# A gated graph layer on one Trainium2 core: the last pair's products reordered, and four loads moved to other places in their queues

## The chip, the cores and the metric

The kernel runs on one core of a Trainium2 chip, in float32. The metric is the device time of one execution in microseconds; the time of a version is the median of its runs. The core has a matrix engine (PE, with PEld for its weight loads), VectorE (DVE), ScalarE (ACT), GpSimd (POOL) and a sync engine (SP) that only issues transfers. SP, ACT and POOL each issue DMAs from their own instruction streams. In this program the transfers of SP and ACT share eight semaphores in rotation: each of them waits, before it is issued, for the landing of the eighth transfer before it. The transfers of POOL have eight of their own.

## The reference, cut to what matters

There are 32 samples of 512 nodes with 256 channels, and a symmetric 0/1 adjacency of 512 x 512 for each.

```python
h = maximum(layernorm(x), 0)                       # per node
xc = transpose(h)                                  # channels x nodes
c = relu(bn1(conv1d(xc, conv1_w)))                 # 1 tap, 256 -> 256
x_conv = relu(bn2(conv1d(c, conv2_w, pad 8)) + xc) # 17 taps, 256 -> 256
s = h @ w_se.T + b_se                              # 3 features a node
A = exp(-|s_n - s_m|^2) * adj
x_nmp = A @ relu(h @ w_msg.T + b_msg)
gi = concat(x_conv, x_nmp) @ w_ih.T + b_ih ; gh = h @ w_hh.T + b_hh
r, z = sigmoid(gi_r + gh_r), sigmoid(gi_z + gh_z)
n = tanh(gi_n + r * gh_n)
out = x + (1 - z) * n + z * h
```

## The kernel before, in words

The samples are worked in two groups of 16, and the gates in 16 pairs after both.

*First part of a group* (`first_part`, L815). For each sample: the load of x (`load_x`, L116, 512 KB; the first sample's x_0 comes in four chunks of 128 KB, L945, by turns on the sync and ScalarE queues), layernorm statistics and normalisation on DVE (L280 to L304, with one power on POOL, L290), transposition on PE (`phT`, L311), the copy of it to DRAM (`hd`, L316), the one-tap convolution (`pc`, L327; DVE L330 makes its output `h`), and the transform of windows of 64 tokens to frequencies (`px`, L342). Between the samples of group 0 the 17-tap weights are transformed to frequencies: `taps`, a 40 KB matrix (its DMA is L133), stays in front of weights `w2p` (DMAs of L242, the first ones on the sync queue, the later ones on POOL's), the products `pw` (L255) are copied to `wst` (L265) and written to DRAM (`wd`). The order of all this is written out by hand (`manual_schedule`). The x of the sample three ahead is loaded at the top of each turn of the loop (L857) into one of three buffers. In group 0 it is on POOL's queue, together with `w2p`; on the sync queue stand the stores `hd` and `wd` and other loads.

*Nodes of a group* (`nodes`, L972). For each sample: message products (`pm`, L439, with DVE L441 and L442 behind them), features and their factors (`psl`, `psr`, `sl`, `sr`, L450 to L467), distances (`pd`, L476), exp on ScalarE (`e`, L479), the adjacency (`load_adj`, L408: four transfers of 256 KB on the sync queue) transposed on DVE in 32 x 32 blocks (`at`, L481), their product `A` (L482), and the aggregate `pn` (L491), which is saved to DRAM. Between them PE works the frequency units of the 17-tap convolution: unit u needs its weights `wt_u` (`load_unit`, L351, two transfers of 256 KB, L354, on the sync queue), their sum on POOL (`wsum`, L358), sums of the transformed input (`both`, L371 and L372, POOL) and makes `py` (L392), `y` (L395 to L400). In this stage the program's scheduler decides the order on each engine and which PSUM bank a tile gets, except for the stretches that are written out. The weights of units 0 to 2 of group 0 are loaded at the end of the first part (L966), ahead of the first adjacency (L984).

*Gates* (L1051 on). A pair's products are made with a scheme of seven products instead of eight, Q1 to Q7 in place of the 2 x 2 blocks of the gates' weights and the two samples: Q1, Q6, Q2, Q7, Q5, Q4, Q3 in this order, each in a PSUM bank of 512 columns, with sums on DVE and sigmoid on ScalarE as banks become ready. The order is written out by hand. For the last pair everything but the z gate's second half is done before; then `last_z` (L653) runs, and nothing comes after it. In it `into` (L601) makes a product, `gated` (L660, L662) adds a sum and takes the sigmoid, `turned` (L669, L672) multiplies with h - n and transposes to token order on DVE, `added` (L677) adds to the output tile, and `store` (L808) issues four transfers of 128 KB for a whole sample, or of 64 KB for half of its columns, by turns on the sync and ScalarE queues. Indices are (channel half, sample of the pair). Q5 and Q3 are computed in two halves of 256 columns, in banks of their own (`b3`); Q4 is computed in one piece in `b4`. Q5 gives the piece (1, 1), Q4 the piece (1, 0), Q3 the piece (0, 1).

Of the kernel before, what the change touches and what calls it, by code (L numbers as in the profile page):

```python
# [65 lines left out]
def gnn_layer(  # L66
# [15 lines left out]
    nc = tc.nc  # L82
# [43 lines left out]
    fwd_np, taps_np, back_np, spans = dft_constants(KT, N)  # L126
# [3 lines left out]
    w1 = early.tile([P, DC, D], FP, name="w1")  # L130
    fwd = early.tile([P, 2 * L], FP, name="fwd")
    taps = early.tile([P, ROWS], FP, name="taps")
    nc.scalar.dma_start(taps, nc.inline_tensor(taps_np, name="dft_taps").ap())  # L133
    back = consts.tile([P, back_np.shape[1]], FP, name="back")

    GC = G // P
# [212 lines left out]
    WT, WSUM, BOTH = {}, {}, {}  # L349
# [158 lines left out]
    Q1, Q6, Q2, Q7, Q5, Q4, Q3 = range(7)  # L508
# [89 lines left out]
    def into(bk, q, o, ks, terms, first, t=slice(0, N)):  # L598

        for i, k in enumerate(ks):  # L600
            nc.tensor.matmul(bk[:, t], sw[:, k, q, o, :], terms[k][q][:, t], start=(first and i == 0), stop=(i == len(ks) - 1),  # L601
                             skip_group_check=True)
# [50 lines left out]
    def last_z(p, terms):  # L653

        d, o, ks = RZ[p], 1, range(K3)

        def gated(src, other, i, j, t=slice(0, N)):
            z, g = d[:, DC + i, j, t], DC + i
            if other is not None:
                nc.vector.tensor_add(z, other[:, t], src[:, t])  # L660
                src = z
            nc.scalar.activation(z, src, AF.Sigmoid, bias=brz[:, g : g + 1], scale=1.0)  # L662

        def places(i, t):
            return slice(t.start // 32, t.stop // 32), slice(32 * i, 32 * (i + 1))

        def turned(i, j, t=slice(0, N)):
            dst, (js, half) = d[:, i, j, t], places(i, t)
            nc.vector.tensor_mul(dst, dst, d[:, DC + i, j, t])  # L669
            if (p, j) not in OUT:  # L670
                OUT[p, j] = pools["late"].tile([P, N // 32, D // 4], FP, tag="o", name=f"o_{p}_{j}", bufs=2)
            nc.vector.transpose(OUT[p, j][:, js, half], dst.rearrange("p (j k) -> p j k", k=32))  # L672

        def added(i, j, t=slice(0, N)):
            js, half = places(i, t)
            x = XP[p][j][:, js, half]
            nc.vector.tensor_add(x, x, OUT[p, j][:, js, half])  # L677


        ts = [slice(h * N // 2, (h + 1) * N // 2) for h in range(2)]  # L680
        b1, b2, b4, *b3 = (bank(f"pz{k}_{p}") for k in range(1, 6))
        into(b1, Q1, o, ks, terms, True)
        p1 = temp("p1", f"z{p}")
        nc.scalar.copy(p1, b1)
        into(b2, Q6, o, ks, terms, True)
        u2 = temp("u2", f"z{p}")
        nc.vector.tensor_add(u2, p1, b2)
        into(b1, Q2, o, ks, terms, False)
        gated(b1, None, 0, 0)
        early_out(p, 1, 1)  # L690
        turned(0, 0)
        into(b2, Q7, o, ks, terms, False)
        u3 = temp("u3", f"z{p}")
        nc.vector.tensor_add(u3, p1, b2)
        early_out(p, 0, 1)
        added(0, 0)
        for bk, t in zip(b3, ts):
            into(bk, Q5, o, ks, terms, True, t)
            gated(bk, u3, 1, 1, t)
        into(b4, Q4, o, ks, terms, True)  # L700
        turned(1, 1)
        added(1, 1)
        gated(b4, u3, 1, 0)
        for bk, t in zip(b3, ts):
            into(bk, Q3, o, ks, terms, False, t)
            gated(bk, u2, 0, 1, t)
            if t is ts[0]:
                turned(1, 0)
        added(1, 0)
        store(p, 0, [nc.sync, nc.scalar])  # L710
        for t in ts:
            turned(0, 1, t)
            added(0, 1, t)
            store(p, 1, [nc.sync, nc.scalar], t)
# [100 lines left out]
    def first_part(g, freq, between, left=()):  # L815


        b0, b1 = g * GB, (g + 1) * GB
        for b in range(b0, b0 + 3):
            if b not in X and (g == 0 or b == b0):  # L820
                load_x(b)
        if g == 0:
            t = XN[b0] = pools["first"].tile([P, NC, D], FP, tag="xn", name="rows", bufs=2)
            ones, diags = t[:, 0, :P], t[:, 1:3, :].rearrange("p i (c m) -> p i c m", m=P)
            nc.vector.memset(ones, 1.0)

            for _ in range(5):
                nc.tensor.matmul(row1[1][:, : 2 * P], ident, fr.rearrange("p c g k -> p (c g k)")[:, : 2 * P], start=True, stop=True)
            batch_norm("bn1", scale1, shift1, nc.gpsimd)
            bn1_row(0, scale1, ones, diags)  # L830
            bn1_row(1, shift1, ones, diags)
        if b0 not in STATS:
            statistics(b0)
        normalise(b0)
        if g == 0:
            scale_w1()
            shift_w1()
        left = list(left)

        def fill():  # L840
            for step in left.pop(0) if left else ():
                step()

        if g > 0:
            load_x(b0 + 1)
            fill()
            load_x(b0 + 2)
        transpose_h(b0)
        fill()
        statistics(b0 + 1)  # L850
        if g > 0:
            statistics(b0 + 2)
        normalise(b0 + 1, g > 0)
        fill()
        for b in range(b0, b1):
            if b + 3 < b1:
                load_x(b + 3, nc.gpsimd)  # L857
            if b == b0:
                conv1(b)
                one, two = between(0) if g == 0 else ([], [])  # L860
                for step in one:
                    step()
                fill()
                if g == 0:
                    transpose_h(b + 1)
                    statistics(b + 2)
                    normalise(b + 2)
                else:
                    normalise(b + 2)
                    transpose_h(b + 1)  # L870
                fill()
                xf, last_two = freq(g), two
                continue
            if g == 0:

                slots = last_two if b == b0 + 1 else between(b - b0)

                def slot():
                    for step in slots.pop(0) if slots else ():
                        step()  # L880

                if b == b0 + 1:
                    between(b - b0)
                    conv1(b)
                    slot()
                if b == b0 + 2:
                    slot()
                if b == b1 - 1:
                    load_h(b0)
                if b + 2 < b1:  # L890
                    statistics(b + 2)
                if b + 1 < b1:
                    transpose_h(b + 1)
                if b > b0 + 2:
                    slot()
                if b + 2 < b1:
                    normalise(b + 2)
                if b > b0 + 1:
                    conv1(b)
                    slot()  # L900
                if b == b1 - 1:
                    by_chunks(b)
                    load_h(b0 + 1)
                windows_to_freq(b - 1, xf)
                slot()
                continue
            if b + 2 < b1:
                statistics(b + 2)
            if b + 1 < b1:
                transpose_h(b + 1)  # L910
            if b + 2 < b1:
                normalise(b + 2)
            one, two = between(b - b0)
            conv1(b)
            if b == b1 - 1:
                load_h(b0)
            for step in one:
                step()
            windows_to_freq(b - 1, xf)
            for step in two:  # L920
                step()
        if g > 0:
            by_chunks(b1 - 1)
            load_h(b0 + 1)
        windows_to_freq(b1 - 1, xf)
        by_chunks(b0)
        return xf
# [8 lines left out]
    with tc.tile_pool(name="freq", bufs=1) as fpool:  # L936
# [3 lines left out]
        with phase("first", "gen"):  # L940
# [7 lines left out]
            load_w1()  # L948
            load_x(1)
            load_taps(gen, 0, nc.sync)  # L950
            nc.scalar.dma_start(fwd, nc.inline_tensor(fwd_np, name="dft_fwd").ap())

            def between(b):
# [9 lines left out]
            with tc.manual_schedule():  # L963
                xf = first_part(0, freq_tile, between)

                for u in range(3):  # L966
                    load_unit(0, u)


# [2 lines left out]
        def nodes(g, xf, units, last):  # L972
# [9 lines left out]
                    features(todo[i])  # L982

            load_adj(todo[0])  # L984
            with tc.manual_schedule():
                begin(0)
                message(todo[1], [0])
                factors(todo[0])
                message(todo[1], [1])
                features(todo[1])  # L990
# [133 lines left out]
```

## Time and profile before

Three runs took 1836.25, 1836.52 and 1836.99 us; the median is 1836.52. The profiled execution has a span of 1835.1 us.

| engine | busy, us | share | instructions |
|---|---|---|---|
| PE | 1814.2 | 99% | 6614 |
| DVE | 1108.7 | 60% | 2220 |
| POOL | 590.5 | 32% | 572 |
| ACT | 583.3 | 32% | 1084 |

The DMA engines moved 289.26 MB. In the first fortieth of the span PE has 8 tenths, in the last 7, in every one between them 9 or more; the DMA share is 8 or 9 tenths in the first seven fortieths (some 320 us), between 5 and 9 in the next twelve, and between 1 and 4 in the last twenty-one.

To read it: busy times are sums over the whole span. A stage's limit is seen in what each engine waited for and in the timeline, whose lines give the start, the length, the engine (with a q at the end for an engine's DMA issues), the line of the code, the operation, the tiles as output<-input and, in brackets, the idle time before and what ended it. A long DMA issue includes the time in which the queue waited for semaphores between several issues that are shown in one line. The columns of a window are the busy time of each engine with its number of instructions, then the clock that was granted to PE (1.00 is full), the mean busy share of the 16 DMA engines and the rate in GB/s.

### The profile page before, as it was taken

What the parts mean: (1) busy time and instruction counts of PE and PEld (TensorE: products, weight loads), DVE (VectorE), ACT (ScalarE), POOL (GpSimd) and SP (SyncE); (2) the same over time, 40 slices, a digit from 0 to 9 for tenths busy, and PEclk for the clock granted to TensorE, in tenths of its full rate; (3) what the DMA queues carried; (4) which work ended last, traced back from release to release, by engine and by line L of the source; (5) the groups of instructions that cost most, each with busy time, mean ns of one, the idle gap of its engine ahead of it and who ended that gap; (6) DMA issues with size and microseconds to landing.
All of it is one profiled execution on the core that took longest, in us unless ns stands there. A gap on an engine that the chain in (4) does not pass through costs nothing.

```text
span 1835.1 us, 20110 instructions
## 1 busy us (share of the span) xinstructions
PE 1814.2 (99%) x6614; PEld 1083.6 (59%) x6614; DVE 1108.7 (60%) x2220; ACT 583.3 (32%) x1084; POOL 590.5 (32%) x572
## 2 busy tenths in 40 slices
PE   8999999999999999999999999999999999999997
PEld 6777666666997766765545554555445554555443
DVE  7884565654995555454266556654666456655666
ACT  4556443432345343333212221222212221222121
POOL 3431333334432534444321332223221323133221
PEclk9999999999999999999999999999999999999999
DMA  9998889775669988767332344224422443234412
GB/s 249 306 299 225 238 225 254 199 208 182 209 225 220 261 249 222 232 194 245 103 111 60 71 121 121 82 38 121 120 87 44 110 121 105 57 79 121 121 27 43
DMA packets 307500, 289.26 MB, mean 158 GB/s; under 512 B 148076, under 2 KB 237196, under 8 KB 307012
## 3 DMA queue, kind: packets, MB, share of 16 engines
q1 hardware_dynamic: 281380, 224.22, 46.2%
q10 hardware_dynamic: 18992, 38.68, 5.9%
q0 software_dynamic: 7024, 25.07, 4.4%
q8 instruction: 53, 0.87, 0.2%
q14 instruction: 51, 0.42, 0.1%
HBM read 191.50 MB, written 96.40 MB: 157 GB/s over the span
## 4 chain that ended last, share of the span: by engine, by line
PE 65%; issue 1%; DVE 1%; POOL 1%; ACT 0%; DVEq 0%; POOLq 0%; ACTq 0%
PE pg L601 30%; PE pn L601 15%; PE pn L491 6%; PE py L392 6%; PE pc L589 5%; PE pm L439 2%; PE pd L476 1%; PE pz L601 1%; PE psr L465 0%; POOL cp L579 0%; POOL nt L791 0%; POOL rz L790 0%; DVE rz L669 0%; DVE o L672 0%; DVE xb L677 0%
## 5 line engine op out<-in xcount | busy, mean ns | idle before, releaser
L491 PE MATMUL pn<-A,msg 128*128 128x512 f32 x512 | 225.7, 593 | 1.2 <-ACT e L479 1.2
L601 PE MATMUL pg<-hp,sw 128*128 128x512 f32 x434 | 221.9, 593 | 0.7 <-DVE rz L620 0.5
L601 PE MATMUL pg<-cp,sw 128*128 128x512 f32 x434 | 221.7, 592 | 0.0
L601 PE MATMUL pg<-np,sw 128*128 128x512 f32 x434 | 221.7, 592 | 0.0
L579 POOL TENSOR_TENSOR hp<-hp 128x512 f32<-128x512 f32 x64 | 82.3, 1296 | 415.9 <-DMA hp<-hd 296.1
L371 POOL TENSOR_TENSOR both<-xf 128x256 f32<-128x256 f32 x78 | 60.6, 777 | 327.2 <-PE py L392 292.5
L491 PEld LDWEIGHTS pn<-A,msg 128*128 128x128 f32 x512 | 96.9, 190 | 111.5 <-issue 105.9
L579 POOL TENSOR_TENSOR cp<-cp 128x512 f32<-128x512 f32 x64 | 80.5, 1268 | 225.6 <-ACT cp L595 224.4
L392 PE MATMUL py<-wt,both 128*128 128x256 f32 x624 | 152.1, 387 | 0.3 <-ACT e L479 0.3
L616 ACT ACTIVATE rz<-rz,brz 128x512 f32<-128x512 f32 x93 | 67.0, 721 | 260.2 <-DVE rz L620 260.2
L399 DVE TENSOR_TENSOR y<-y,py 128x256 f32<-128x256 f32 x78 | 31.8, 408 | 186.6 <-ACT y L398 182.6
L601 PEld LDWEIGHTS pg<-hp,sw 128*128 128x128 f32 x434 | 82.4, 190 | 104.6 <-issue 97.7
L601 PEld LDWEIGHTS pg<-cp,sw 128*128 128x128 f32 x434 | 82.6, 190 | 103.7 <-issue 103.7
L601 PEld LDWEIGHTS pg<-np,sw 128*128 128x128 f32 x434 | 82.6, 190 | 103.7 <-issue 103.7
L392 PEld LDWEIGHTS py<-wt,both 128*128 128x128 f32 x624 | 114.9, 191 | 43.1 <-issue 28.3
L482 DVE TENSOR_TENSOR A<-e,at 128x512 f32<-128x512 f32 x128 | 114.5, 933 | 32.8 <-ACT e L479 32.6
L358 POOL TENSOR_TENSOR wsum<-wt 128x512 f32<-128x512 f32 x78 | 108.5, 1392 | 49.9 <-DMA wt<-wd 37.3
L739 ACT ACTIVATE nt<-nt,vech 128x512 f32<-128x512 f32 x64 | 46.2, 722 | 235.8 <-DVE nt L738 235.8
L327 PE MATMUL pc<-w,hT 128*128 128x256 f32 x512 | 117.9, 384 | 1.1 <-DVE hT L315 1.1
L439 PE MATMUL pm<-wmsg,hq 128*128 128x259 f32 x512 | 117.5, 382 | 0.0
L601 PE MATMUL pn<-hp,sw 128*128 128x512 f32 x224 | 114.4, 592 | 0.0
L601 PE MATMUL pn<-np,sw 128*128 128x512 f32 x224 | 114.4, 592 | 0.0
(145 smaller groups left out, 2946.4 us busy)
## 6 DMA issues: line engine op xcount, KB each, us to landing
wt<-wd SPq DMA_DIRECT2D x160, 256.0 KB, 4.4
adj<-in_adj_dram SPq DMA_DIRECT2D x128, 256.0 KB, 5.6
wd<-wst SPq DMA_DIRECT2D x64, 320.0 KB, 6.4
yd<-y ACTq DMA_DIRECT2D x80, 256.0 KB, 4.1
yt<-yd SPq DMA_DIRECT2D x30, 640.0 KB, 7.5
hd<-hT SPq DMA_DIRECT2D x32, 512.0 KB, 4.9
nd<-nmp ACTq DMA_DIRECT2D x32, 512.0 KB, 4.3
xb<-in_x_dram SPq DMA_DIRECT2D x128, 128.0 KB, 3.8
```

The costliest lines, as they stand in the source:

```text
L327: nc.tensor.matmul(p[:, j, :], HT[b][:, ic, c * P : (c + 1) * P], w1[:, ic, :], start=(ic == 0), stop=(ic == DC - 1))
L358: nc.gpsimd.tensor_tensor(t, WT[g, u][:, 0], WT[g, u][:, 1], op=ALU.add)
L371: nc.gpsimd.tensor_tensor(both[:, 0], re, im, op=ALU.add)
L392: nc.tensor.matmul(dst, v[:, ic, :], w[:, ic, :], start=(ic == 0), stop=(ic == DC - 1))
L439: nc.tensor.matmul(p[:, : D + NS], hq[:, ic, c * P : (c + 1) * P], wmsg[:, ic, :], start=(ic == 0), stop=(ic == DC - 1))
L482: nc.vector.tensor_mul(A[b][:, mc, :], e, at)
L491: nc.tensor.matmul(p, MSG[b][:, mc, dc * P : (dc + 1) * P], A[b][:, mc, :], start=(mc == 0), stop=(mc == NC - 1))
L579: nc.gpsimd.tensor_tensor(t[:, dst, :], t[:, a, :], t[:, b, :], op=sub)
L589: nc.tensor.matmul(bk[:, t0:t1], YT[p][j][:, c, oc * P : (oc + 1) * P], back[:, n : n + t1 - t0], start=(c == 0), stop=(c == len(spans) - ...
L601: nc.tensor.matmul(bk[:, t], sw[:, k, q, o, :], terms[k][q][:, t], start=(first and i == 0), stop=(i == len(ks) - 1), skip_group_check=True)
L616: nc.scalar.activation(rz[:, g, j, :], src, AF.Sigmoid, bias=brz[:, g : g + 1], scale=1.0)
L739: nc.scalar.activation(n, n, AF.Tanh, bias=b_in[:, i : i + 1], scale=1.0)
```

## The change

It has four parts.

1. In `last_z` Q4 is computed in front of Q5's two halves instead of behind them. The piece (1, 0) is turned after Q5's first half and added after Q5, and the first sample of the pair is stored there; the piece (1, 1) is turned after Q3's first half and added after Q3. The same instructions are issued in another order. Its purpose is to have the first sample of the pair complete earlier, so that its stores are not in front of the last ones.
2. The DMA of `taps` goes behind the two chunks of x_0 on ScalarE's queue, so that x_0 comes first.
3. The loads of x_3, x_4 and x_5 go from POOL's queue to the sync queue, where each stands between the stores of `hd`.
4. The weights of the third unit (`wt_2`) are loaded behind the first adjacency instead of in front of it. In group 1 they are there already and the condition is false.

In the nodes' stage of group 0 the scheduler's order changes with the fourth part: at its start DVE's work for `y_1`, `y_2` and the next sample's `st` and `msg` stands in front of the second adjacency's `at` and `A`, POOL's `wsum_2` behind `both_3`, and PSUM banks are given out otherwise, so that some `pd`, `py` and `pn` wait for other readers of their bank. The order of PE's instructions is the same in both but for `last_z`, and each engine has as many instructions as before, apart from the three loads.

```diff
@@ -130,7 +130,6 @@
     taps = early.tile([P, ROWS], FP, name="taps")
-    nc.scalar.dma_start(taps, nc.inline_tensor(taps_np, name="dft_taps").ap())
     back = consts.tile([P, back_np.shape[1]], FP, name="back")
@@ -694,20 +693,21 @@
         early_out(p, 0, 1)
         added(0, 0)
+        into(b4, Q4, o, ks, terms, True)
+        gated(b4, u3, 1, 0)
         for bk, t in zip(b3, ts):
             into(bk, Q5, o, ks, terms, True, t)
             gated(bk, u3, 1, 1, t)
-        into(b4, Q4, o, ks, terms, True)
-        turned(1, 1)
-        added(1, 1)
-        gated(b4, u3, 1, 0)
+            if t is ts[0]:
+                turned(1, 0)
+        added(1, 0)
+        store(p, 0, [nc.sync, nc.scalar])
         for bk, t in zip(b3, ts):
             into(bk, Q3, o, ks, terms, False, t)
             gated(bk, u2, 0, 1, t)
             if t is ts[0]:
-                turned(1, 0)
-        added(1, 0)
-        store(p, 0, [nc.sync, nc.scalar])
+                turned(1, 1)
+        added(1, 1)
         for t in ts:
             turned(0, 1, t)
             added(0, 1, t)
             store(p, 1, [nc.sync, nc.scalar], t)
@@ -854,7 +854,7 @@
             if b + 3 < b1:
-                load_x(b + 3, nc.gpsimd)
+                load_x(b + 3, nc.sync if b < 3 else nc.gpsimd)
@@ -948,6 +948,7 @@
             load_taps(gen, 0, nc.sync)
+            nc.scalar.dma_start(taps, nc.inline_tensor(taps_np, name="dft_taps").ap())
             nc.scalar.dma_start(fwd, nc.inline_tensor(fwd_np, name="dft_fwd").ap())
@@ -963,7 +964,7 @@
-                for u in range(3):
+                for u in range(2):
                     load_unit(0, u)
@@ -982,6 +983,8 @@
             load_adj(todo[0])
+            if (g, 2) not in WT:
+                load_unit(g, 2)
             with tc.manual_schedule():
```

## The prediction, made before the changed kernel was run

> **What bounds the kernel now.** I read the page's busy times first, then what TensorE (PE) waited for, then the timeline around each of those waits, then windows of 3.4 us for the clock, and last the timeline of the end.
>
> ```profile
> PE 1814.2 (99%) x6614; PEld 1083.6 (59%) x6614; DVE 1108.7 (60%) x2220; ACT 583.3 (32%) x1084; POOL 590.5 (32%) x572
> ```
>
> PE is busy 1814.2 of 1835.1 us. The other 20.9 us are all that reordering can give back, apart from matmuls that ran at a lower clock: 1.9 before the first matmul, about 8.1 in gaps, 10.9 after the last matmul has ended (1824.2). What PE waited for (total, times, longest):
>
> ```profile
> PE pn L491 <- ACT e L479: 1.2, 1, 1.2
> PE px L342 <- DVE h L330: 1.2, 1, 1.2
> PE phT L311 <- DVE xn L303: 1.2, 1, 1.2
> ```
>
> These are single events, all in the first 180 us. The second, from the timeline (start, length, engine, line, idle before):
>
> ```profile
> 20.25 0.81 POOL L118 DMA_DIRECT2D x<-in_x_dram  x1
> ...
> 30.70 1.40 DVE L284 BATCH_NORM_STATS2 stats<-x 128x6 f32<-128x256 f32 x4 [2.04 <-DMA x<-in_x_dram]
> ...
> 33.24 1.41 PE L342 MATMUL px<-fwd,h 128*128 128x160 f32 x8 [0.48 <-DVE hT L315]
> ...
> 35.85 1.41 PE L342 MATMUL px<-fwd,h 128*128 128x160 f32 x8 [1.20 <-DVE h L330]
> ```
>
> The fifth sample's load (x_4) is issued by GpSimd (POOL) at 20.25, lands at 30.67, and VectorE (DVE) stands 2.04 us in front of its statistics. DVE's later work is late by that, and PE waits 0.48 + 1.20 for it. The first wait of the list:
>
> ```profile
> 176.84 1.30 DVE L481 STREAM_TRANSPOSE at<-adj 128x512 f32<-128x512 f32 x2 [1.32 <-DMA adj<-in_adj_dram]
> ...
> 179.65 7.13 PE L491 MATMUL pn<-A,msg 128*128 128x512 f32 x16 [1.24 <-ACT e L479]
> ```
>
> The first adjacency's last quarter lands at 176.71, DVE waits 1.32 for it, and the chain transpose, exp, A, first aggregate brings 1.24 of it to PE. The windows behind (PE, PEld, DVE, ACT, POOL busy; then PEclk, DMA share, GB/s):
>
> ```profile
> 193.10:196.50 3.40, 2.72 (x11) 0.88 (x10) 3.40 (x15) 1.98 (x4) 0.73 (x1) 1.00 1.17 201
> 196.50:199.90 3.40, 3.40 (x10) 2.68 (x10) 3.40 (x5) 2.35 (x5) 0.72 (x2) 0.53 1.21 185
> ```
>
> In the second PE has a clock of 0.53: 3.4 x 0.47 = 1.6 us lost without being idle. The end:
>
> ```profile
> 1823.60 0.59 PE L601 MATMUL pz<-cp,sw 128*128 128x256 f32 x2
> 1824.05 0.69 DVE L669 TENSOR_TENSOR rz<-rz 128x512 f32<-128x512 f32 x1 [0.46 <-ACT rz L662]
> ...
> 1826.42 4.90 SPq L808 DMA_DIRECT2D out_dram<-xb  x6
> 1826.42 5.09 ACTq L808 DMA_DIRECT2D out_dram<-xb  x6
> ...
> 1828.52 0.42 DVE L677 TENSOR_TENSOR xb<-xb,o 128x256 f32<-128x256 f32 x1
> ```
>
> After PE's end DVE works without a break to 1828.94 and six stores on each queue follow.
>
> [...] all 16 DMA engines have a share of 0.9 to 1.0 from 10 to 40 us. [...] The 64 KB stores at the end take 2.7 to 4.3 us to landing. [...] The trace shows one window at half rate, [...] after a thin stretch (nine-row matmuls, a gap of 0.68).
>
> **The change part by part.**
>
> *Tail.* Same instructions, another order. PE goes on without a gap: Q4 (six matmuls of 512, 2.58 us) from 1816.28 to 1818.86, Q5's halves to 1820.15 and 1821.44, Q3's as before to 1822.73 and 1824.02. DVE: fourth add 1819.06 to 1819.75; first Q5 half added at 1820.8, its mul and transpose (1.00 + 0.71 for 512 columns at these lines[...]) to 1822.2; second half added at 1822.6; the output add (0.65) to 1823.2. In before that output add ended at 1826.39: the first sample's four stores leave 3.2 us earlier. Then come Q3's two adds (0.4 each) and, for three half-sized pieces, mul, transpose and add (0.42 + 0.45 + 0.43, with issue 1.4 each): DVE has no rest from 1822.6, and its last add ends near 1828.5 instead of 1828.94, that is 0.4 earlier. The last stores gain more. Before, they were issued at 1830.1 to 1831.2, up to 2.3 us after their data, since each transfer of the two hardware queues waits for the landing of the eighth before it, and the first sample's stores had left only at 1826.4 to 1827.7. Now those land by about 1827.5, before 1828.5. The last issue, second of two in a row on its queue (0.45 each), then starts near 1829.0 and lands 2.7 to 3.5 later, at 1831.7 to 1832.5 instead of 1833.9; the end came 1.2 after that landing. Gain 1.4 to 2.2; I take 1.8. The added costs: two store issues on ScalarE (0.39 + 0.46) now stand in front of Q3's two sigmoids, which then end near 1824.6 and 1826.0, while DVE comes to them at 1826.1 and 1827.4: nothing. PE's second Q3 half needs DVE's read of the second Q5 half, 1822.6 against PE's 1822.73: nothing, by 0.1.
>
> *Taps behind x.* One issue of 0.46 leaves ScalarE's front; chunks 1 and 3 of x_0 land 0.45 earlier (4.50 and 5.64 before). The first layernorm chain follows, but at 14.05 PE waits for the taps' weights w2p from the sync queue, which don't move. Gain 0.1 to 0.4; 0.2. Taps itself, 40 KB wanted at 14, is hidden.
>
> *x_3 to x_5 on the sync queue.* POOL loses three issues (1.00, 0.81, 0.80), off the path. x_4 stands behind the second hd store (issue about 18), 2 us earlier than now and in front of the 128 KB w2p that preceded it on POOL. Landing between 25 and 30, as 512 KB shares full engines; DVE wants it at 28.65. So of the 1.68 us on PE, 0.3 to 1.68 goes; I take 1.4. New wait: x_5 now stands behind the hd store of 27.22, so leaves at about 28.5 instead of 25.93, and lands near 36 instead of 33.38, while its statistics are wanted at about 34.5 once x_4 is on time. DVE then stands 1.5 to 2.3 us; behind it are transposes and PSUM copies for a PE that has 2 to 3.7 us of such work ready. Cost 0 to 1; 0.3. Head together: -0.2 - 1.4 + 0.3 = -1.3 (-2.0 to -0.1). From 40 to 165 us PE has no gap, though DVE stands up to 1.72 there, so shifts in that stretch cost nothing.
>
> *Adjacency in front of the third weights.* Two transfers of 256 KB, some 1.3 us each by the distance between the adjacency's landings (172.86, 174.18, 175.54, 176.71), move behind. The last quarter lands at about 174.1, and DVE is then bound by its own work, which ends at 175.51: 1.32 earlier, so PE's 1.24 go. The third weights land at about 176.7 instead of 171.5; POOL wants them at about 178, PE at 187: free. -1.2.
>
> *The scheduler's side effect.* In that stage DVE now does the y sums and the next sample's msg before the second adjacency's transposes, and PSUM banks are dealt otherwise: distance (pd), y and aggregate matmuls wait for other readers. From the end of the second message batch (193.43) to the next aggregate (200.61) before took 7.18. With the new order I count two small gaps (0.25 and 0.95, on exps) instead of 0.68, and no half-rate window: 4.9. [...] half of -2.3: -1.1.
>
> Sum: -1.8 - 1.3 - 1.2 - 1.1 = -5.4; with the median before of 1836.5 this gives 1831.1, rounded to 1831.0.
>
> **Rivals.** *Only the certain half*: tail -1.8, adjacency -1.2, head -0.1 (x_5 takes back what x_4 gives, PE waits for w2p), no gain at 193: -3.1, 1833.4, inside 0.2%. For it: DMA engines are full in the head[...]. Against: x_4 was late by its place in the queue, and that is mended. *All of it*: head -2.0, adjacency -1.2, tail -1.9, 193 us -2.3: -7.4, 1829.1. For it: [...] gaps get smaller. Against: new gaps at the same place. *Slower*: the tail's early end is worth its 0.4 only[...]; x_5's stall reaches PE in full (+2); the new bank order stalls PE on exps in several samples and each thin stretch is followed by a half-rate window (+1.6 each, three of them): +6.4 in all with adjacency and tail off, about 1841.5. For it: one such window is in the trace. Against: DVE is busy 60%, and from 204 us on PE waits next to nothing.
>
> **How the numbers follow.** Forecast 0.52, certain half 0.26, all of it 0.16, slower 0.06. 0.2% is 3.7 us: under 1832.85 is faster. The forecast's spread crosses that bound now and then (0.05), the certain half is mostly same: faster 0.74, same 0.20, slower 0.06. The range reaches from all of it (1829.0) to just over the certain half (1834.0).
>
> **What would show it.** Right: DVE's output add for the first sample ends near 1823.2 before the end's shift, last stores without waiting, 9 us from PE's last matmul to the end; px without waits at 33 and 36; pn's first wait gone; PEclk 1.0 at 196. Wrong: a DVE stall on x_5 that is followed by a PE gap, PE waits at py or pd near 195, a new window at half rate, or the last stores landing as long after the last add as before.

## The result and the profile after

The changed kernel takes 1832.05 us (median of 6 runs, 1828.42 to 1835.48); the kernel before 1836.81 (6 runs). The ratio is 0.9971 with an interval of 0.9958 to 0.9984: 5.3 us faster, between 2.9 and 7.7. Taken a second time it was 1830.34 against 1836.32, ratio 0.9964 (0.9950 to 0.9977). The prediction of 1831.0 lies between both times.

Single runs of one version differ by several us, so a part worth one or two us does not show by time alone. I therefore took the span apart at four events of PE that are in the same place of its order in every version: the first distance product `pd`, the first aggregate `pn`, the second sample's `pn`, and the end of PE's last matmul ("PE's end" below). Worked out from the times in the traces (us, the kernel before and the changed kernel in two profiles each, the second ones from the runs further down):

| stretch | before | before, again | after | after, again |
|---|---|---|---|---|
| start to first pd | 167.29 | 165.87 | 166.42 | 165.32 |
| first pd to first pn | 12.36 | 13.05 | 12.65 | 12.64 |
| first pn to second pn | 20.96 | 20.91 | 18.63 | 19.62 |
| second pn to PE's end | 1623.59 | 1623.23 | 1624.25 | 1622.85 |
| PE's end to the end | 10.88 | 10.83 | 8.05 | 8.16 |
| span | 1835.08 | 1833.89 | 1830.01 | 1828.59 |

The page's busy times after:

```profile
PE 1815.0 (99%) x6614; PEld 1083.9 (59%) x6614; DVE 1107.4 (61%) x2220; ACT 583.8 (32%) x1084; POOL 588.6 (32%) x569
```

PE's work is what it was (1814.2 before); what shrank is the rest, from 20.9 to 15.0 us. What PE waited for after the change (total, times, longest):

```profile
PE pd L475 <- ACT sr L466: 1.0, 1, 1.0
PE pn L490 <- DVE A L481: 0.9, 1, 0.9
PE pc L326 <- DVE hT L314: 0.8, 2, 0.5
PE pw L254 <- DMA w2p<-in_w2T_dram: 0.7, 1, 0.7
```

All three waits that the prediction shows of before are gone. In their place stand one for `sr` that was 0.62 before, one for `A` at 860 us that the first profile of before does not have, and one for `w2p` at 13.3 us, which the prediction named as what eats the earlier x_0. The head's timeline, in which the load at 28.29 is that of x_5 (x_4's left at 17.54 and landed at 26.37):

```profile
28.29 1.29 SPq L118 DMA_DIRECT2D x<-in_x_dram  x1
29.01 1.39 DVE L283 BATCH_NORM_STATS2 stats<-x 128x6 f32<-128x256 f32 x4
...
34.80 2.44 PE L341 MATMUL px<-fwd,h 128*128 128x160 f32 x16
```

No stall in front of x_4's statistics and none in front of `px`. Yet the stretch to the first pd is only 0.9 shorter. The windows show one reason, a stretch at half clock at 28.0 (PE, PEld, DVE, ACT, POOL busy, then PEclk, DMA share, GB/s):

```profile
24.59:28.00 3.41, 3.41 (x16) 1.59 (x16) 3.38 (x13) 3.07 (x8) 1.01 (x1) 1.00 1.02 335
28.00:31.41 3.41, 3.41 (x13) 2.96 (x12) 3.38 (x13) 0.00 (x0) 0.38 (x1) 0.50 0.97 284
164.53:167.94 3.41, 2.40 (x15) 1.18 (x14) 1.46 (x9) 3.41 (x9) 0.00 (x0) 1.00 1.07 332
167.94:171.35 3.41, 3.41 (x12) 2.87 (x11) 0.00 (x0) 1.60 (x4) 1.27 (x1) 0.50 1.25 190
```

The stretch at half clock that stood at 196.7 us before is not there; two others are, at 28.0 and 167.9, the second of them behind the first pd. In the first aggregate's timeline the wait for the adjacency is gone from the first line, and the gap from the second:

```profile
176.29 1.31 DVE L480 STREAM_TRANSPOSE at<-adj 128x512 f32<-128x512 f32 x2
...
179.07 7.03 PE L490 MATMUL pn<-A,msg 128*128 128x512 f32 x16
```

The end:

```profile
1820.11 0.68 DVE L676 TENSOR_TENSOR xb<-xb,o 128x512 f32<-128x512 f32 x1
...
1820.81 5.96 SPq L808 DMA_DIRECT2D out_dram<-xb  x6
1820.81 0.94 ACTq L808 DMA_DIRECT2D out_dram<-xb  x2
...
1821.36 0.59 PE L600 MATMUL pz<-cp,sw 128*128 128x256 f32 x2
...
1824.72 2.13 ACTq L808 DMA_DIRECT2D out_dram<-xb  x4
...
1825.49 0.43 DVE L676 TENSOR_TENSOR xb<-xb,o 128x256 f32<-128x256 f32 x1
```

The first sample's stores now leave at 1820.81, 1.1 us ahead of PE's last matmul's end (1821.95), not 2.2 behind it. By the issue and landing times of the transfers, the last of them starts at 1826.37, 0.45 behind the end of the last add, and not at 1831.19, 2.25 behind it; from there to landing it takes as long as before (2.6 and 2.7).

### The profile page after: what moved, and what is told of

The parts are those of the page before. It is cut to its first block, busy times and chain, and to the rows that moved or that the text cites. A ratio compares the mean times of both kernels' runs of the same rounds, so it can differ in the third digit from the quotient of the medians.

```text
span 1830.0 us, 20109 instructions
## 1 busy us (share of the span) xinstructions
PE 1815.0 (99%) x6614; PEld 1083.9 (59%) x6614; DVE 1107.4 (61%) x2220; ACT 583.8 (32%) x1084; POOL 588.6 (32%) x569
## 4 chain that ended last, share of the span: by engine, by line
PE 65%; issue 1%; DVE 1%; POOL 1%; ACT 0%; DVEq 0%; POOLq 0%; ACTq 0%
PE pg L600 30%; PE pn L600 15%; PE pn L490 6%; PE py L391 6%; PE pc L588 5%; PE pm L438 2%; PE pd L475 1%; PE pz L600 1%; PE psr L464 0%; DVE A L481 0%; POOL cp L578 0%; POOL nt L791 0%; POOL rz L790 0%; DVE at L480 0%; DVE o L671 0%
## 5 line engine op out<-in xcount | busy, mean ns | idle before, releaser
L600 PE MATMUL pn<-cp,sw 128*128 128x512 f32 x224 | 114.4, 592 | 0.0
```

## The experiments

### Each part alone

The kernel before with the changed `last_z` (the first part of the change as shown above), with the adjacency in front, with x on the sync queue, and with taps behind x_0:

```diff
@@ tail
+        into(b4, Q4, o, ks, terms, True)
+        gated(b4, u3, 1, 0)
...
+        added(1, 0)
+        store(p, 0, [nc.sync, nc.scalar])
@@ adjacency
-                for u in range(3):
+                for u in range(2):
...
             load_adj(todo[0])
+            if (g, 2) not in WT:
+                load_unit(g, 2)
@@ x
-                load_x(b + 3, nc.gpsimd)
+                load_x(b + 3, nc.sync if b < 3 else nc.gpsimd)
@@ taps
-    nc.scalar.dma_start(taps, nc.inline_tensor(taps_np, name="dft_taps").ap())
...
             load_taps(gen, 0, nc.sync)
+            nc.scalar.dma_start(taps, nc.inline_tensor(taps_np, name="dft_taps").ap())
```

> The kernel before with the new order of the last pair's z gate alone. Theory: from the end of PE's last matmul to the end of the program 8.1 us, as in the changed kernel, instead of 10.9; everything ahead of it as before, so 1836.5 - 2.8 = about 1833.7, ratio 0.9985. Rival: the stores' landing in the changed kernel was helped by the other parts (fewer transfers, other phases), and the order alone brings only the earlier last add, 0.4 to 0.8 us: about 1835.9.

> The kernel before with the first adjacency in front of the third weights alone. Theory: PE's gap of 1.24 in front of the first aggregate goes, and from the second message batch to the second aggregate 0.4 to 0.7 us of gaps go too: 1.7 us less by gaps, about 1834.8. A further 1.6 comes or goes with each stretch of 3.4 us at half clock, which need not sit at 196.7 us any more. Rival: the reordered VectorE work and the other PSUM banks cost as much as the gap, and the saving at 193 to 200 us in the changed kernel was only the absence of the half-rate stretch: 1.2 less at most by gaps, about 1835.3.

> The kernel before with x_3, x_4 and x_5 on the sync queue alone. Theory: VectorE's 2.04 us wait for x_4 at 28.7 shrinks under 1 and PE's gaps of 0.48 and 1.20 at 33 and 36 us go; 1.0 to 1.7 less if no stretch at half clock falls into the first 40 us: about 1835.1. Rival: x_5, now behind the store of hd, makes VectorE wait over 1.5 us at about 35 us, and the gap only moves: 1836.5.

> The kernel before with the taps' matrix behind x_0 alone. Theory: layernorm of the first sample 0.4 to 0.8 us earlier, but PE waits for w2p at 14.0 us as before, so PE's gain by 14.1 us is below 0.1: 1836.5, no change. Rival: the earlier first sample reaches the second sample's chain on VectorE and GpSimd, and 0.3 to 0.5 remains behind 14 us: 1836.1.

Against the kernel before (median 1837.47 of 49 runs) the ratios are: tail 0.9997 (0.9988 to 1.0007), adjacency 0.9990 (0.9983 to 0.9997), x 0.9996 (0.9988 to 1.0004), taps 1.0003 (0.9990 to 1.0016). By time only the adjacency is told from no change, at 1.8 us (0.6 to 3.1). By the stretches of their profiles:

| stretch | tail | adjacency | x | taps |
|---|---|---|---|---|
| start to first pd | 167.70 | 165.44 | 167.97 | 166.86 |
| first pd to first pn | 13.34 | 10.95 | 12.08 | 12.46 |
| first pn to second pn | 20.97 | 18.63 | 19.27 | 20.95 |
| second pn to PE's end | 1624.70 | 1625.25 | 1624.59 | 1626.28 |
| PE's end to the end | 8.31 | 10.53 | 10.56 | 10.76 |

The tail's 2.5 us stand in the last row, as its theory had it; its time is the rival's, and its interval (at most 2.2 us faster) just leaves 2.5 out. The adjacency's expectation is met in rows two and three. For taps PE again waits at 13.4 us for w2p (0.64), and no gain is to be seen in the time. With x on the sync queue DVE's wait moves to x_5 and is shorter than its rival's 1.5; PE has no gap over 0.3 between 20 and 160 us. Its time is not told from no change either:

```profile
30.59 1.39 DVE L284 BATCH_NORM_STATS2 stats<-x 128x6 f32<-128x256 f32 x4
...
37.69 1.41 DVE L284 BATCH_NORM_STATS2 stats<-x 128x6 f32<-128x256 f32 x4 [0.86 <-DMA x<-in_x_dram]
```

### Both kernels once more

> The kernel before, unchanged, profiled a second time: how much of what its first profile showed belongs to every execution. In the profiles of three versions that load x_3 to x_5 on GpSimd's queue as the kernel before does, PE's gaps of 0.48 and 1.20 behind x_4 were absent. Theory: x_4's landing is a matter of the single execution, and so are the stretches at half clock: here the gaps at 33 and 36 us are absent or under 0.5 in sum, the gap of about 1.2 in front of the first aggregate is there, the end is 10.5 to 11 us behind PE's last matmul. Rival: the head's gap is regular in this kernel and the other parts took it away in those versions: 1.2 to 1.7 again.

The kernel before, unchanged, in a second profile:

```profile
29.65 1.39 DVE L284 BATCH_NORM_STATS2 stats<-x 128x6 f32<-128x256 f32 x4
...
33.83 2.44 PE L342 MATMUL px<-fwd,h 128*128 128x160 f32 x16
```

The wait of 2.04 for x_4 and both `px` gaps are absent: x_4 landed at 27.52, not 30.67. It did so in every other profile with these loads on GpSimd's queue (26.95 to 27.96). So the head's largest gap shows in the first profile of before alone. The gap in front of the first aggregate is there (1.93), and the end comes 10.83 us after PE's.

> The changed kernel, unchanged, profiled and timed again in more rounds. Theory: the sum of the parts by gaps, some 2.7 at the end, 1.2 to 1.7 at the first aggregates, under 0.5 in the head, is 4.0 to 5.0 us and the median is 1832.5 to 1833.5; its profile has the first aggregate without a gap over 0.3 and ends about 8.1 us after PE's last matmul, with stretches at half clock in places other than 28.0 and 167.9. Rival: the parts help each other (the profile of the first run), 5.5 or more, median below 1832.

1830.34, ratio 0.9964: by time the rival's number and not the theory's. By stretches (first table) its parts are like those of the first profile. It has a single stretch at half clock in place of two, at 167.1, and so nearly where one of them was. The gap in front of the first aggregate is gone again, and the end is 8.16 us behind PE's.

### Without the tail, and without x

The changed kernel with the old `last_z`, and with the old loads:

```diff
@@ no tail
-        into(b4, Q4, o, ks, terms, True)
-        gated(b4, u3, 1, 0)
         for bk, t in zip(b3, ts):
             into(bk, Q5, o, ks, terms, True, t)
             gated(bk, u3, 1, 1, t)
...
+        into(b4, Q4, o, ks, terms, True)
+        turned(1, 1)
+        added(1, 1)
+        gated(b4, u3, 1, 0)
@@ x on GpSimd's queue
-                load_x(b + 3, nc.sync if b < 3 else nc.gpsimd)
+                load_x(b + 3, nc.gpsimd)
```

> The changed kernel with the last pair's z gate in its old order: parts 2, 3 and 4 together, without part 1. Theory: the end is 10.5 to 10.9 us behind PE's last matmul instead of 8.1 and the time 2.6 above the changed kernel's: ratio to before 0.9978 to 0.998, about 1833 if before is 1836.5. Rival: part 1 is worth no more than its own timing alone said (1.2 us by the means of 13 and 49 runs), so the rest brings more: ratio 0.997 to 0.9975.

> The changed kernel with x_3 to x_5 back on GpSimd's queue: parts 1, 2 and 4. Theory: part 3 is worth next to nothing, since in four of five profiles of kernels with these loads on GpSimd's queue x_4 had landed by 28.0 us and VectorE did not wait, and on the sync queue VectorE waits 0.2 to 0.9 us for x_3 or x_5 instead: within 0.5 us of the changed kernel, ratio 0.9962 to 0.9968, PE at the end of the first 40 us (its 180th matmul) within 0.7 of the changed kernel's 37.8 to 38.5 where no stretch at half clock falls in front of it. Rival, the prediction's step: 1.1 us slower than the changed kernel, the 180th matmul at 39 to 40 us, VectorE waiting about 2 us for x_4.

Without the tail: 1832.88, ratio 0.9972 (0.9962 to 0.9983), and 10.46 us from PE's end to the end. By time this sits with the rival, by the profile with the theory; the interval holds both. Without x on the sync queue: 1831.68, ratio 0.9968 (0.9956 to 0.9979), with the first pd at 165.56 and no wait of DVE for x_4. That is within 0.5 us of the changed kernel, as the theory had it: the moved loads bring nothing that shows.

### What shortens the end

The changed kernel with the issue of the stores alone behind the piece (1, 1), and with the output add in front of them there as well:

```diff
@@ late store
         added(1, 0)
-        store(p, 0, [nc.sync, nc.scalar])
...
         added(1, 1)
+        store(p, 0, [nc.sync, nc.scalar])
@@ late add
-        added(1, 0)
-        store(p, 0, [nc.sync, nc.scalar])
...
         added(1, 1)
+        added(1, 0)
+        store(p, 0, [nc.sync, nc.scalar])
```

> The changed kernel with the first sample's four stores issued behind the piece (1, 1) instead of in front of it: two positions later in the program, about 2.5 us, where they stood in the kernel before by VectorE's order. Theory: what shortens the end is that the last stores no longer wait for these to land; with late stores they wait again, and the end comes 9.5 to 10.5 us after PE's last matmul instead of 8.1, although VectorE's last add ends 4.0 us after it as in the changed kernel. Rival: the time from the last add to the end (4.1 instead of 6.2) is a matter of what else is on the DMA queues, not of this order: 8.1 to 8.6.

The expectation failed, by the way the experiment was made: the end is 8.06 us behind PE's (1830.46 us, ratio 0.9966). The sync engine issued its first store 0.03 us behind the output add (1819.47 after 1819.44; 0.02 in the changed kernel, 1820.81 after 1820.79), so its stores did not move at all; ScalarE's left some 2 us later (1821.48) and had landed all the same by 1824.42, before the last add ended (1824.58). The late add delays the data themselves:

> The changed kernel with the first sample's last output add, and so its stores, behind the piece (1, 1): their data are ready 2.5 to 3 us later, which moving the issue alone did not bring about. VectorE does the same work, so its last add still ends 4.0 us after PE's last matmul. Theory: the last eight stores wait again for these four to land, since each transfer of these queues waits for the eighth before it: the end is 5.2 to 6.0 us behind the last add, 9.2 to 10 behind PE, instead of 4.1 and 8.1. Rival: the stores' landing at the end depends on the work of the queues only: 4.1 to 4.5 and 8.1 to 8.5.

```profile
1824.71 4.89 SPq L808 DMA_DIRECT2D out_dram<-xb  x6
1824.71 5.09 ACTq L808 DMA_DIRECT2D out_dram<-xb  x6
...
1826.81 0.43 DVE L676 TENSOR_TENSOR xb<-xb,o 128x256 f32<-128x256 f32 x1
```

The end comes 5.60 us after the last add and 10.17 after PE's end; the time is 1833.22, ratio 0.9977 (0.9969 to 0.9985). The last stores' issues start at 1828.4 to 1829.5, up to 2.25 us behind the end of the last add (1827.23), with the landings of the first sample's four stores between 1827.4 and 1829.5 ahead of them. The last two of these issues start 0.02 and 0.07 us after such a landing (1829.46 and 1828.99), as in the kernel before, where they start 0.02 and 0.06 after (1831.17 and 1830.69). That is the picture of the kernel before. The last add ends 4.57 us after PE's end, where the expectation had 4.0: the output add that stands late is 0.68 us which in the changed kernel fits in while DVE would wait for PE. So the tail's 2.5 us are two things: DVE work that is done while PE still works, and the waits of the last stores. By means over the profiles with the new and the old order the last add ends 3.96 and 4.74 us after PE's end (0.8), and the end comes 4.17 and 5.93 after the last add (1.8). The last issue starts 0.45 to 0.58 us behind the last add in all seven with the new order, and 2.23 to 2.27 in all six with the old.

### ScalarE's queue at the first distances, and the clock

The changed kernel with the copies of hq behind, and with a longer gap:

```diff
@@ hq behind
                 features(todo[1])
+                if todo[2] not in HQ:
+                    by_chunks(todo[2])
@@ longer gap (again is 2 for the first sample of group 0, else 0)
-        nc.scalar.copy(by_chunk(t), chunks(p))
+        for _ in range(1 + again):
+            nc.scalar.copy(by_chunk(t), chunks(p))
```

> The changed kernel with the copies of the third sample's hq on ScalarE put behind sl and sr of the first (one line more in the written order of the nodes' start). Theory: PE's gap of 0.6 to 1.0 in front of the first pd at 165 us is ScalarE's queue: hq waits there for a load that lands at 163.4, and relu, sl and sr stand behind it. With it gone the gap is below 0.2, 0.6 to 1.0 us less: ratio to the kernel before about 0.0005 below that of the changed kernel, at the edge of what can be told by time. Rival: sr is late by its input, and the gap stays.

The gap in front of the first pd is gone (1.0 in the changed kernel), which shows that sr was late by its place behind hq on ScalarE. The time is 1830.82, ratio 0.9968 (0.9957 to 0.9980): not told from the changed kernel.

> The changed kernel with sr of the first sample copied three times instead of once (the same values written again), which lengthens PE's gap in front of the first distances at 165 us from 1.0 to about 2.5 us; in the other direction than the version with hq behind, whose gap there was gone and which had no stretch at half clock behind it. Theory: a thin stretch of PE's work brings the next 3.4 us to half clock: the profile has one that starts between 166 and 171, and the median is 1.5 (the gap) plus 0.5 to 1.7 above the changed kernel's, 1832.5 to 1833.7. Rival: stretches at half clock come by themselves and not from gaps; none there or by chance, and 1.5 above: 1832.

```profile
PE pd L476 <- ACT sr L467: 2.3, 1, 2.3
...
PE pd L476 <- ACT e L479: 0.7, 1, 0.7
```

1836.54, ratio 0.9993 (0.9986 to 1.0000): 4 to 5 us slower than the changed kernel by the ratios, more than either expectation. And no stretch at half clock starts between 166 and 171, so the theory failed; the one there is starts at 197.8:

```profile
194.35:197.76 3.41, 2.68 (x9) 1.37 (x9) 3.41 (x17) 2.26 (x4) 1.82 (x1) 1.00 0.71 155
197.76:201.17 3.41, 3.41 (x9) 2.60 (x8) 3.41 (x5) 1.75 (x4) 1.84 (x2) 0.50 1.18 271
```

The run is not a clean one: with two copies more the scheduler went back to nearly the order of before for DVE's work at 193 us, and the gap of `pd` on `e` that belongs to it (0.7) came back. By stretches it has 21.79 from the first to the second pn, where the changed kernel has 18.63 and 19.62. The gap (1.3 more than in the changed kernel) and this stretch (2.2 to 3.2 more, the one at half clock in it) make 3.5 to 4.5 us. The run thus says little about gaps and the clock. That the old order is the dearer one fits it, but does not follow from it alone, since up to 1.7 of the stretch, half of 3.41, can be the half clock.

## Why the prediction was right

The time, the direction and the sum were right: 5.4 us were predicted, 5.3 (2.9 to 7.7) measured. The terms of the sum were not all of the predicted size: the head brought next to nothing and the tail more than was counted, so that the nearness of the two numbers is in part luck. Means over all profiles, with a part against without it:

| term | predicted | by the profiles | from |
|---|---|---|---|
| tail | -1.8 | -2.5 | PE's end to the end: 8.13 in seven profiles, 10.67 in the six with the old order (8.00 to 8.36 and 10.46 to 10.88) |
| head | -1.3 | -0.2, not told from zero | first pd: 166.38 in six with taps and x moved and one copy of sr (165.3 to 167.3), 166.58 in four with neither (165.4 to 167.7) |
| adjacency | -1.2 | -1.4 by gaps, -0.9 on the mean | first pd to first pn: 11.21 in the five with one copy of sr and the clock full, 11.75 in all eight, 12.66 in the five without |
| side effect | -1.1 | -1.0 | first to second pn: 19.58 in the same eight, 20.61 in five |

Together -4.6 on the mean. From the second pn to PE's end those eight and those five both have 1624.5, so nothing came from there. PE's last 100 matmuls take 38.2 us in all fourteen profiles: the new order of the tail does not move PE's end. In the prediction's slower rival a sum is off: 2 and 4.8 less the 0.4 of the tail and the 1.2 of the adjacency make 5.2, some 1841.7, where it has 6.4 and 1841.5.

**Tail: the mechanism was right, the size too small.** DVE's last add comes 0.8 earlier against PE's end, where 0.4 were counted: the prediction took 1.00 for the first multiplication of 512 columns, and it took 0.68. Before, it ran beside GpSimd's last sum; in the new order it stands just behind that sum (first two lines before, the others after):

```profile
1817.87 2.71 POOL L786 TENSOR_TENSOR xb<-xb,on 128x1024 f32<-128x1024 f32 x1 [6.03 <-DVE on L797]
1820.13 1.00 DVE L669 TENSOR_TENSOR rz<-rz 128x512 f32<-128x512 f32 x1 [0.65 <-ACT rz L662]
...
1815.63 2.71 POOL L786 TENSOR_TENSOR xb<-xb,on 128x1024 f32<-128x1024 f32 x1 [6.03 <-DVE on L797]
1818.45 0.68 DVE L668 TENSOR_TENSOR rz<-rz 128x512 f32<-128x512 f32 x1
```

The two lengths are the same in every profile of either order. The waits of the stores gave 1.8, against the 1.4 that were left for them; the predicted "last stores without waiting" is in the trace, and the late add brings the waits back. (From the start of its issue to its landing a store of the last eight took 2.4 to 2.7 us in the changed kernel's first profile, by the seven whose landing the trace tells.) What stays open is why the tail is worth less by time, alone (0.9997, at most 2.2 us) and by what the changed kernel loses without it (0.9972 against 0.9964 to 0.9971): in the profile of the tail alone PE ended at 1826.71, later than in the two profiles of before (1824.19 and 1823.06), after two stretches at half clock; whether that is chance was not shown.

**Head: this step failed.** The prediction read PE's gaps of 0.48 and 1.20 as a property of the queue's order. The second profile of before has neither, so the -1.4 for x_4 had nothing to take away. In all eight profiles with these loads on the sync queue DVE waits for one of them: for x_5 in five (0.40 to 0.86, not the 1.5 to 2.3 of the prediction), for x_3 in three (0.65 to 0.80). But PE has no gap over 0.32 between 20 and 160 us in any of them, so this cost nothing that shows. That PE would wait at w2p was as predicted. The range that was given for the head, -2.0 to -0.1, was too narrow by the step's own terms: the least of the gains and the whole of the cost add up to +0.6.

**Adjacency: right.** The gap of 1.2 is gone in seven of the nine profiles with this part and 0.41 and 0.46 in two, where the five others have 0.96 to 2.23. DVE is bound by its own work at 176.3, as worked out. What the step lacked is that three of the nine profiles with this part have a stretch at half clock right behind the first distances (from 167.1 to 167.9), which takes back 1.4; none of the five others has. Whether the part brings it about was not tested.

**Side effect: right in sum, by a split that was a guess.** In the changed kernel's first profile the gaps were 0.27 and none. In its second profile, and in two experiments, `py` waits 1.0 to 1.3 for `e`, the 0.95 of the prediction. Half-rate stretches near 195 us did not vanish: two of the eight profiles with the new order have one, three of the five with the order of before, and the run with the longer gap, which is back at that order, too.

**A new wait.** The 0.93 at 860 us, after the change:

```profile
858.42 4.28 POOL L578 TENSOR_TENSOR np<-np 128x512 f32<-128x512 f32 x3 [1.12 <-DMA np<-nd]
858.58 1.66 DVE L481 TENSOR_TENSOR A<-e,at 128x512 f32<-128x512 f32 x1
860.29 1.98 PE L490 MATMUL pn<-A,msg 128*128 128x512 f32 x4 [0.93 <-DVE A L481]
```

and the same place before:

```profile
861.78 0.69 DVE L482 TENSOR_TENSOR A<-e,at 128x512 f32<-128x512 f32 x1
861.80 4.47 POOL L579 TENSOR_TENSOR np<-np 128x512 f32<-128x512 f32 x3 [1.30 <-DMA np<-nd]
```

The order of the two engines' work is the same. In this profile after the change GpSimd's sum of two tiles started 0.16 us ahead of DVE's product and the product took 1.66; before it started 0.02 behind it and the product took 0.69. In eleven of the fourteen profiles GpSimd's sum starts first, by 0.14 to 0.76, and the product then takes 1.06 to 1.68 and ends 1.8 us after the sum's start each time; in the three in which it starts second the product takes 0.69. Why the product takes longer behind the sum's start was not shown. GpSimd's sum starts when a load lands (it had waited 1.12 us for it after the change and 1.30 before), and with that the order of the two can change. So the wait comes and goes from profile to profile: 0.33 in the second profile of before, none in the second of after, 0.74 to 0.83 in three experiments with the order of before. It is no cost of the change.

## What to carry to other kernels

At the end of a kernel look at when the last transfers are issued, not only at when their data are ready: stores that left late held up later ones here through the semaphores that they share, so that the last issue started 2.23 to 2.27 us behind its data with the old order and 0.45 to 0.58 with the new; pulling an earlier output forward took 2.5 us off the end here, of which the times alone show less. A gap in one profile that hangs on a transfer's landing (x_4 at 30.67 in one profile of before, at 27.52 in the other) needs a second profile before it is counted as a gain. And where a change is worth 0.3% and runs scatter by as much, compare stretches between fixed instructions, not times.

## What was not expected of the hardware

The clock of PE halved here without PE being idle: it went to 0.50 at 28.0 us in the changed kernel, behind 3.41 us in which PE was busy throughout. In the fourteen profiles a clock of 0.50 sets in sixteen times ahead of the last 20 us, fifteen times for 3.41 us and once for twice that. Sorted by what PE did in the window of 3.41 us just before, worked out from the starts and ends of its matmuls: in fourteen of the sixteen, matmuls with all 128 rows filled less than half of the window (0.16 to 0.49), the rest being gaps and the 9-row `pd` or 17-row `pw` products. In the changed kernel the window ahead of 28.0 us is 29% full products and 71% `pw`.

This is no rule. With the spans cut into windows of 3.41 us in step with these stretches, some forty other windows with less than half passed without it, all of them with a full share of 0.30 or more; two stretches at 10.8 us follow windows of 0.66, and the second half of the double one follows a window of 0.79 at half clock. No experiment varied the thin products alone.

Nor do gaps alone tell it: at 165 us gaps of 0.9 to 1.1 had such a stretch behind them in three profiles of four, and one of 2.3 had none. What brings a stretch about was not shown. By estimate one costs at most 1.7 us, half of its 3.41, which is a good part of the scatter between runs: of the 49 runs of before that stood beside the single parts, those with a mean clock of 0.998 took 1836.3 on the mean, 0.997 1837.5, 0.995 and 0.996 1839.1.
